# A selective-scan kernel: diagonal matrices read from spaced DRAM rows, softplus summed by accumulating DMAs, y added to DRAM by a DMA

## The chip, the core and the metric

The kernel runs on one core of one Trainium2 chip. The metric is the device time of one execution in microseconds, as the median of several. The engines named below are TensorE (PE, with its weight loads shown apart as PEld), VectorE (DVE), ScalarE (ACT), GpSimd (POOL) and SyncE (SP), which here only issues DMAs. Each engine executes its own instructions in the order in which they are written, and waits on semaphores for the others.

## The reference, cut to what matters

Two layers act on an image of 256 x 256 tokens with 128 channels: an attention over rows, then a state-space layer in the manner of VMamba. The change lies in the second layer, in its selective scan. Four scans (rows forward, columns forward, and both backward) run over the 65,536 tokens, with 256 inner channels d and 16 states n:

```python
delta = jax.nn.softplus(dts + dt_bias)
def step(h, inp):
    d_t, x_t, B_t, C_t = inp
    dA = jnp.exp(d_t[..., None] * As)
    h = dA * h + (d_t * x_t)[..., None] * B_t[:, :, None, :]
    y = jnp.einsum('bkdn,bkn->bkd', h, C_t)
    return (h, y)
...
y = out_y[:, 0] + inv_y[:, 0] + wh_y + invwh_y
```

So for each token: a step size delta for each channel, a decay exp(delta A) for each channel and state, an input delta x B, a recurrence, and a sum over the 16 states weighted with C. The four directions are added up token by token.

## The kernel before, in words

Seven stages follow one another: statistics, a norm, attention, the convolution, a transposition of one array in DRAM, the four scans, and the output. The scans take most of the time and they alone are changed. Everything is float32.

A scan is cut into 64 blocks of 1024 tokens (`TB`); four scans make 256 blocks. In each block there are 32 units, one for each state m (16) and each half h of the channels (2 x 128). A unit is written as s in the program, with s = 2m + h. The program is ordered by hand (`manual_schedule`): `body` (L908) walks over the units, and in each unit it writes for each engine the work that is due.

- `recur` (L853): DVE runs the recurrence of one unit as one scan instruction over 1024 tokens (L858), from the decay `da` and the input `mm` (a PSUM tile). After h = 1, DVE saves the last state (L863), and POOL multiplies both halves of the result `hs` with C of this state (`cc`, L865).
- `turn` (L841): PE makes the input of the unit one ahead, delta x B, as channels on partitions and tokens along the row. For four of the eight groups of 128 tokens (`DJ = NJ // 2`) it multiplies delta x (`dxt`) by a diagonal matrix `dg` that has B on its diagonal (L846). For the other four, ACT has scaled `dxt` by B into `but` and PE only transposes (L848). There are two such PSUM tiles (`mms`), so `turn` of unit u + 1 can run once the scan of unit u - 1 is over.
- `scale` (L830): ACT makes `dg` (the identity, scaled row by row, L833) and `but` (L835), six units ahead, in rings of four.
- `decay` (L837): ACT makes `da`, four units ahead, in a ring of six.
- `collect` (L869): PE transposes the products `hs` back and adds them up in PSUM tiles `y` over the 16 states, at least three states (`LAG`) behind, at most ten transposes in a unit unless `share` (L906) names another number.
- `fetch` (L825): SP loads `cc` for a state (512 KB, one row spread over 128 partitions) into a ring of four. It waits until POOL has multiplied with the buffer's former contents.
- `begin` (L737): the pieces that prepare the next block while the present one is scanned, each with the unit at which it is written. In units 6 and 8 PE forms the pre-activation of delta (`rate`, L745, into a tile of `mms`) and ACT takes its absolute value (`size`). Then ACT forms exp(-|v|), the logarithm log(1 + e), and a rounding correction (units 9 to 12). POOL adds the three parts (L780, L777, units 11 to 14). In units 18 and 20 PE forms the pre-activation again, and DVE adds max(v, 0) to give `delta` (L783). In units 22 and 24 PE transposes `delta` (`turn_rate`, L785) and DVE multiplies by x (`times_x`, L792) to give `dxt`.
- `evict` (L893): in units 6 and 8 of the next block, DVE adds the PSUM sums of a block to `yb` (L898). That buffer was loaded from `y` in DRAM at unit 16 (L948) and is stored back by SP (L902).

The order of SP's queue is the order of writing; a DMA that has to wait holds up those written after it.

Of the kernel before, what the change touches and what calls it, by code (L numbers as in the profile page):

```python
# [29 lines left out]
AF = mybir.ActivationFunctionType  # L30
ALU = mybir.AluOpType
# [588 lines left out]
def scans(tc, io, c):  # L620
# [19 lines left out]
    with tc.tile_pool(name="e_w", bufs=1) as wp, tc.tile_pool(name="e_1", bufs=1) as sb1, tc.tile_pool(  # L640
# [11 lines left out]
        def ring(name, n, shape, pool=wp):  # L652
            return [pool.tile(shape, F32, name=f"{name}{i}") for i in range(n)]

        DJ = NJ // 2
        xks = ring("xk", 1, [P, NJ, DI])

        dts = ring("dt", 1, [P, TB])
# [7 lines left out]
        bus = ring("but", 4, [P, NJ - DJ, DI])  # L666
# [18 lines left out]
        class Block:  # L685
# [40 lines left out]
            def load_tokens(self):  # L726
                nc.sync.dma_start(out=self.as_rows(self.bt), in_=self.rows(io["bk"][self.S.k]))
                nc.sync.dma_start(out=self.as_rows(self.xk), in_=self.rows(io["xk"]))

            def advance(self, now, after):  # L730
                if self.pieces is None:
                    self.pieces = begin(self)
                while self.pieces and self.pieces[0][:2] <= (now, after):
                    _, _, f, *args = self.pieces.pop(0)
                    f(*args)

        def begin(B):  # L737
# [19 lines left out]

            def size(h):
                nc.scalar.activation(B.e[:, h, :], B.pu[h], AF.Abs)  # L759

            def exp():
                nc.scalar.activation(B.e, B.e, AF.Exp, scale=-1.0)
# [10 lines left out]

                nc.scalar.activation(B.w, B.w, AF.Identity, scale=-1.0, bias=1.0)

            def less(h):
                nc.gpsimd.tensor_tensor(B.lw[:, h, :], B.lw[:, h, :], B.w[:, h, :], ALU.add)  # L777

            def log1p(h):
                nc.gpsimd.tensor_tensor(B.lw[:, h, :], B.lw[:, h, :], B.e[:, h, :], ALU.add)  # L780

            def softplus(h):
                nc.vector.scalar_tensor_tensor(B.delta[:, h, :], B.pu[h], 0.0, B.lw[:, h, :], ALU.max, ALU.add)  # L783

            def turn_rate(i):  # L785
                B.pt = mm().rearrange("p (j d) -> p j d", d=DI)
# [5 lines left out]
            def times_x(i):  # L792
# [5 lines left out]
                    ALU.mult,  # L798
                )

            return [
                (6, False, rate, 0),
                (6, True, size, 0),
                (8, False, rate, 1),
                (8, True, size, 1),
                (9, True, exp),
                (10, True, log),
                (11, True, log1p, 0),
                (11, True, one_plus),
                (12, True, log1p, 1),  # L810
                (12, True, rest),
                (13, True, less, 0),
                (14, True, less, 1),

                (18, False, rate, 0),
                (18, True, softplus, 0),
                (20, False, rate, 1),
                (20, True, softplus, 1),
                (22, False, turn_rate, 0),
                (22, True, times_x, 0),  # L820
                (24, False, turn_rate, 1),
                (24, True, times_x, 1),
            ]

        def fetch(B, m):  # L825
            nc.sync.dma_start(out=ccs[m % 4], in_=B.S.C[m : m + 1, B.where()].partition_broadcast(P))

        def scale(B, m, h):  # L830
            dg, bu = dgs[m % 4], bus[m % 4]
            for j in range(h * DJ // 2, (h + 1) * DJ // 2):
                nc.scalar.activation(dg[:, j, :], c.ident, AF.Copy, scale=B.bt[:, B.slot(j), m : m + 1])  # L833
                at = B.slot(DJ + j)
                nc.scalar.activation(bu[:, j, :], B.dxt[:, DJ + j, :], AF.Copy, scale=B.bt[:, at, m : m + 1])  # L835

        def decay(B, m, h):  # L837
            da = das[((B.n * DS + m) * NH + h) % DA]
# [2 lines left out]
        def turn(B, m, h):  # L841
            d1 = B.d1 = mm()
            dg, bu = dgs[m % 4], bus[m % 4]
            hc = slice(h * P, (h + 1) * P)
            for j in range(DJ):
                nc.tensor.matmul(d1[:, j * P : (j + 1) * P], B.dxt[:, j, hc], dg[:, j, :], start=True, stop=True)  # L846
            for j in range(DJ, NJ):
                nc.tensor.transpose(d1[:, j * P : (j + 1) * P], bu[:, j - DJ, hc], c.ident)  # L848
            d1s.append(d1)

        d1s = []
# [41 lines left out]
        def evict(B, after, part):  # L893

            n = NJ // PB // 2
            for g in range(part * n, (part + 1) * n):
                to = B.y[:, g * PB : (g + 1) * PB, :]
                nc.vector.tensor_tensor(to, to, pys[g], ALU.add)  # L898
                if after:
                    after.free.add(g)  # L900
            if part == 1:
                nc.sync.dma_start(out=B.rows(io["y"]), in_=B.as_rows(B.y))  # L902

        U = NH * DS

        share = {6: 0, 7: 8, 8: 0, 18: 3, 20: 3, 22: 5, 24: 5}  # L906

        def body(blocks, before, after):  # L908

# [11 lines left out]
            def do(f, u):  # L921
                if at(u):
                    f(*at(u))

            if before is None:
                blocks[0].load()
                blocks[0].load_tokens()
                blocks[0].advance(U, True)
                blocks[0].free = set(range(NJ // PB))
                blocks[1].load()  # L930
                for m in range(4):
                    fetch(blocks[0], m)
                for u in range(3 * NH):
                    do(scale, u)
                for u in range(4):
                    do(decay, u)
                do(turn, 0)
            for x, B in enumerate(blocks):
                nxt = at_hand.get(x + 1)
                for s in range(U):  # L940
                    u = x * U + s
                    m, h = divmod(s, NH)
                    if s == 0 and nxt:
                        nxt.load_tokens()
                    if s == 21 and x + 2 in at_hand:
# [12 lines left out]
                    if nxt:  # L958
                        nxt.advance(s, True)
                    do(decay, u + 4)  # L960
                    if u == 0:
                        nc.scalar.preload_act_table_set("natural_log_exp_and_others")
                    do(scale, u + 3 * NH)
                    if h == NH - 1 and at(u + 1 + 3 * NH):
                        fetch(*at(u + 1 + 3 * NH)[:2])
            if not after:
                waiting.extend((*at(u), j) for u in range(own * U - LAG * NH, own * U) for j in range(NJ))
                collect_some(len(waiting))
                for part in range(2):
                    evict(blocks[-1], None, part)  # L970
            assert not waiting


# [24 lines left out]
def output(tc, io, c):  # L998
# [73 lines left out]
    "dc1": (KD // 2 * RC, NT),  # L1072
    "dcT": (KD // 2 * RC, NT),
    "y": (NT, DI),
}


# [56 lines left out]
```

## Time and profile before

| what | value |
|---|---|
| median of 3 runs | 28445.06 us (28438.65 to 28445.41) |
| profiled execution, first to last instruction | 28447.5 us |
| stretch of the four scans (4744 to 27715 us) | 22971 us, that is 89.7 us for each of 256 blocks |
| busy in that stretch: PE, DVE, ACT, POOL | 21791, 21224, 22282, 21572 us |
| the same for one block | 85.1, 82.9, 87.0, 84.3 us |
| share of the 16 DMA engines, and rate, in that stretch | 0.39, 131 GB/s |
| granted TensorE clock, mean of the span | 0.965 |

The profiled execution is within 0.01% of the median of the runs, so its times can be set against the runs directly. Busy time is the time in which an instruction of an engine is under way; successive ACT instructions overlap a little, so that the distance from start to start (the pitch) is the shorter measure of what one costs.

### The profile page before, as it was taken

Reading aid. Unit: us, or ns where it says so; the run is one execution under the profiler, and the core shown is the slowest. Engines: PE = TensorE matmul, PEld = TensorE weight load, DVE = VectorE, ACT = ScalarE, POOL = GpSimd, SP = SyncE. Lnnn points to the kernel's source line nnn. Section 1 sums busy time; section 2 is a strip of 40 time slices with the busy share of each in tenths; the row PEclk is TensorE's granted clock in tenths of the full one; section 3 lists DMA queues with packets and bytes.
Section 4 is the critical chain, followed back from the end, with each engine's and each line's share of the span. In section 5 each row is a group of like instructions: output and inputs, shape, how many; then the busy total and the mean of one; then the engine's idle time right before and its main releaser. Section 6 shows DMA issues by size and latency. Waiting matters only on the chain. (4 is left out here: it accounts for less than half of the span.)

```text
span 28447.5 us, 528099 instructions
## 1 busy us (share of the span) xinstructions
PE 26610.1 (94%) x196490; PEld 22529.2 (79%) x196490; DVE 24922.2 (88%) x24253; ACT 25332.4 (89%) x49673; POOL 22944.4 (81%) x10118
## 2 busy tenths in 40 slices
PE   8999996999999999999999999999999999999998
PEld 3555444888888888888888888888888888888884
DVE  4777665999999999999999999999999999999987
ACT  6875224999999999999999999999999999999987
POOL 2443002999999999999999999999999999999983
PEclk9999998999999999999999999999999999999999
DMA  5112345433433333333334333333333333333335
GB/s 206 55 50 71 111 116 115 132 132 129 133 130 133 132 131 132 132 131 132 128 132 133 131 133 132 131 132 129 132 132 130 133 132 129 132 130 132 133 132 172
DMA packets 1923996, 3630.07 MB, mean 128 GB/s; under 512 B 532297, under 2 KB 1240009, under 8 KB 1889490
## 3 DMA queue, kind: packets, MB, share of 16 engines
q1 hardware_dynamic: 1424722, 3339.77, 34.6%
q10 hardware_dynamic: 496640, 255.88, 3.2%
q8 instruction: 1568, 25.69, 0.4%
q14 instruction: 1066, 8.73, 0.1%
HBM read 3002.42 MB, written 592.84 MB: 126 GB/s over the span
## 5 line engine op out<-in xcount | busy, mean ns | idle before, releaser
L865 POOL TENSOR_TENSOR hs<-hs,cc 128x1024 f32<-128x1024 f32 x8192 | 19202.5, 2380 | 1346.1 <-DVE state L863 679.9
L858 DVE TENSOR_TENSOR_SCAN hs<-da,state,mm 128x1024 f32<-128x1024 f32 x8192 | 18976.6, 2340 | 1465.4 <-PE mm L848 1074.7
L846 PE MATMUL mm<-dg,dxt 128*128 128x128 f32 x65536 | 9305.0, 287 | 1065.1 <-DVE hs L858 886.1
L846 PEld LDWEIGHTS mm<-dg,dxt 128*128 128x128 f32 x65536 | 8328.4, 199 | 2257.9 <-DVE hs L858 1897.8
L839 ACT ACTIVATE da<-delta,A 128x1024 f32<-128x1024 f32 x8192 | 9328.4, 1139 | 112.2 <-PEq L984 76.0
L617 PE MATMUL y<-ident,hs 128*128 128x128 f32 x65536 | 8511.4, 275 | 1.4 <-POOL hs L865 1.4
L835 ACT ACTIVATE but<-dxt,bt 128x256 f32<-128x256 f32 x16384 | 8150.2, 497 | 11.4 <-DVE dxt L794 11.4
L617 PEld LDWEIGHTS y<-ident,hs 128*128 128x128 f32 x65536 | 7494.1, 143 | 1.9 <-POOL hs L865 1.9
L833 ACT ACTIVATE dg<-ident,bt 128x128 f32<-128x128 f32 x16384 | 6393.1, 390 | 0.2
L848 PE MATMUL mm<-ident,but 128*128 128x128 f32 x32768 | 5092.5, 280 | 0.0
L848 PEld LDWEIGHTS mm<-ident,but 128*128 128x128 f32 x32768 | 4011.4, 146 | 0.0
L750 PE MATMUL mm<-dt,dtw 9*128 9x512 f32 x4096 | 2033.0, 615 | 265.9 <-DMA bt<-mid_bk 184.5
L385 POOL TENSOR_TENSOR an<-ex,rs 128x1024 f32<-128x1024 f32 x512 | 970.2, 1895 | 1024.5 <-PE tp L394 566.3
L780 POOL TENSOR_TENSOR lw<-lw,e 128x1024 f32<-128x1024 f32 x512 | 1207.7, 2384 | 336.3 <-ACT lw L766 336.3
L750 PEld LDWEIGHTS mm<-dt,dtw 9*128 9x128 f32 x4096 | 680.7, 184 | 959.5 <-issue 733.3
L500 POOL MEMSET pad<- 128x10 f32 x32 | 3.7, 117 | 1650.0 <-PE ps L537 1639.9
L777 POOL TENSOR_TENSOR lw<-lw,w 128x1024 f32<-128x1024 f32 x512 | 1202.9, 2375 | 0.0
L537 PE MATMUL ps<-pad,w 128*128 128x512 f32 x2048 | 954.8, 610 | 161.0 <-ACT xi L525 161.0
L372 ACT ACTIVATE ex<-sc,nm 128x256 f32<-128x256 f32 x2048 | 1013.7, 499 | 0.4
L759 ACT ACTIVATE e<-mm 128x1024 f32<-128x1024 f32 x512 | 524.7, 1025 | 522.1 <-PE mm L750 521.9
L355 DVE CUSTOM_DVE_ANT_0 sc<-ps,bias 128x256 f32<-128x256 f32 x2048 | 746.2, 421 | 117.3 <-PE ps L340 117.3
L394 PEld LDWEIGHTS tp<-ident,an 128*128 128x128 f32 x4096 | 467.5, 141 | 470.7 <-POOL an L385 235.1
(137 smaller groups left out, 18522.4 us busy)
## 6 DMA issues: line engine op xcount, KB each, us to landing
cc<-mid_dc SPq DMA_DIRECT2D x2048, 512.0 KB
cc<-mid_dcT SPq DMA_DIRECT2D x2048, 512.0 KB
xk<-mid_xk SPq DMA_DIRECT2D x256, 1024.0 KB
yb<-mid_y SPq DMA_DIRECT2D x256, 1024.0 KB
mid_y<-yb SPq DMA_DIRECT2D x256, 1024.0 KB
xt<-mid_xT SPq DMA_DIRECT2D x64, 1024.0 KB
mid_xk<-xk ACTq DMA_DIRECT2D x32, 2048.0 KB
mid_y<-y ACTq DMA_DIRECT2D x32, 2048.0 KB
```

Source lines behind the costliest of these rows:

```text
L372: nc.scalar.activation(exs[u][:, x, :], scs[u][:, e, jt, :], AF.Exp, scale=-1.0, bias=nms[u][:, e, jt : jt + 1], accum_out=sms[u][:, x : x ...
L617: nc.tensor.matmul(out, in_, c.ident, is_transpose=True, start=start, stop=stop, skip_group_check=True)
L750: nc.tensor.matmul(pu[:, q : q + T], dtw[0 : DR + 1, k, h * P : (h + 1) * P], B.dt[0 : DR + 1, q : q + T], start=True, stop=True,)
L777: nc.gpsimd.tensor_tensor(B.lw[:, h, :], B.lw[:, h, :], B.w[:, h, :], ALU.add)
L780: nc.gpsimd.tensor_tensor(B.lw[:, h, :], B.lw[:, h, :], B.e[:, h, :], ALU.add)
L833: nc.scalar.activation(dg[:, j, :], c.ident, AF.Copy, scale=B.bt[:, B.slot(j), m : m + 1])
L835: nc.scalar.activation(bu[:, j, :], B.dxt[:, DJ + j, :], AF.Copy, scale=B.bt[:, at, m : m + 1])
L839: nc.scalar.activation(da, B.delta[:, h, :], AF.Exp, scale=A[:, B.S.k * NH + h, m : m + 1])
L846: nc.tensor.matmul(d1[:, j * P : (j + 1) * P], B.dxt[:, j, hc], dg[:, j, :], start=True, stop=True)
L848: nc.tensor.transpose(d1[:, j * P : (j + 1) * P], bu[:, j - DJ, hc], c.ident)
L858: nc.vector.tensor_tensor_scan(o, d0, d1, state[:, m, h : h + 1], ALU.mult, ALU.add)
L865: nc.gpsimd.tensor_tensor(hs[:, x, :], hs[:, x, :], ccs[m % 4], ALU.mult)
```

## The change

1. **Diagonals.** `DJ` becomes 3: the groups 0, 2 and 4 go by a diagonal, the other five by scaling and a transposition. ACT no longer makes `dg`. Instead a new piece `spread` is written in units 10, 13, 16 and 19 for four states each: ACT copies 12 columns of B into a zeroed tile `z` at a spacing of 128 elements, and SP writes the whole tile (128 rows of 1664 elements, 0.85 MB) to DRAM (`apart`, two copies by the parity of the block). Reading that with a row step one element shorter than the row shifts each row by one element, which yields the three diagonal matrices of a state: `diagonal`, one SP load of 0.2 MB for each state, into the same ring `dg`.
2. **Softplus.** ACT writes max(v, 0) into `delta` by Relu right after the Abs, and the three further parts are added onto `delta` by three DMAs that accumulate, issued from POOL in units 12, 15 and 18, 1 MB each from SBUF to SBUF. The second `rate`, POOL's four additions and DVE's `softplus` are gone.
3. **y.** The sums are copied out of PSUM by ACT instead of being added by DVE, and a DMA from POOL in unit 10 (`add_y`) accumulates them onto `y` in DRAM. The load of `yb` at unit 16 and SP's store are gone.

```diff
-        DJ = NJ // 2
+        DJ = 3
+        BJ = NJ - DJ
+        by_diagonal, by_scale = (0, 2, 4), (1, 3, 5, 6, 7)
+        GS = 4
+        ZL = P * (GS * DJ + 1)
...
+        zs = ring("z", 1, [P, ZL])
+        for z in zs:
+            nc.vector.memset(z, 0.0)
...
             def size(h):
                 nc.scalar.activation(B.e[:, h, :], B.pu[h], AF.Abs)
+                nc.scalar.activation(B.delta[:, h, :], B.pu[h], AF.Relu)
...
-            def less(h):
-                nc.gpsimd.tensor_tensor(B.lw[:, h, :], B.lw[:, h, :], B.w[:, h, :], ALU.add)
-
-            def log1p(h):
-                nc.gpsimd.tensor_tensor(B.lw[:, h, :], B.lw[:, h, :], B.e[:, h, :], ALU.add)
-
-            def softplus(h):
-                nc.vector.scalar_tensor_tensor(B.delta[:, h, :], B.pu[h], 0.0, B.lw[:, h, :], ALU.max, ALU.add)
+            def add(name):
+                nc.gpsimd.dma_start(out=B.delta, in_=getattr(B, name), accum_op=ALU.add)
...
+            def spread(g):
+                z = zs[0]
+                first, step = B.slot(by_diagonal[0]), B.slot(by_diagonal[1]) - B.slot(by_diagonal[0])
+                nc.scalar.copy(
+                    z[:, P - 1 : P - 1 + GS * DJ * P].rearrange("p (m j q) -> p j m q", j=DJ, q=P)[:, :, :, 0],
+                    B.bt[:, first : first + step * (DJ - 1) + 1 : step, g * GS : (g + 1) * GS],
+                )
+                nc.sync.dma_start(out=B.apart(g), in_=z)
+
+            pieces = [(10 + 3 * g, True, spread, g) for g in range(DS // GS)]
+            return sorted(pieces + [
                 (6, False, rate, 0),
                 (6, True, size, 0),
                 (8, False, rate, 1),
                 (8, True, size, 1),
                 (9, True, exp),
                 (10, True, log),
-                (11, True, log1p, 0),
                 (11, True, one_plus),
-                (12, True, log1p, 1),
                 (12, True, rest),
-                (13, True, less, 0),
-                (14, True, less, 1),
-
-                (18, False, rate, 0),
-                (18, True, softplus, 0),
-                (20, False, rate, 1),
-                (20, True, softplus, 1),
+                (12, True, add, "lw"),
+                (15, True, add, "e"),
+                (18, True, add, "w"),
                 (22, False, turn_rate, 0),
...
+        def diagonal(B, m):
+            of = B.apart(m // GS)
+            of = bass.AP(of.tensor, of.offset + P - 1 + m % GS * DJ * P, ((ZL - 1, P), (1, DJ * P)))
+            nc.sync.dma_start(out=dgs[m % 4].rearrange("p j q -> p (j q)"), in_=of)
...
-            for j in range(h * DJ // 2, (h + 1) * DJ // 2):
-                nc.scalar.activation(dg[:, j, :], c.ident, AF.Copy, scale=B.bt[:, B.slot(j), m : m + 1])
-                at = B.slot(DJ + j)
-                nc.scalar.activation(bu[:, j, :], B.dxt[:, DJ + j, :], AF.Copy, scale=B.bt[:, at, m : m + 1])
+            for x in range(h * BJ // 2, (h + 1) * BJ // 2):
+                j = by_scale[x]
+                nc.scalar.activation(bu[:, x, :], B.dxt[:, j, :], AF.Copy, scale=B.bt[:, B.slot(j), m : m + 1])
...
-                nc.vector.tensor_tensor(to, to, pys[g], ALU.add)
+                nc.scalar.copy(to, pys[g])
...
+        def add_y(B):
+            nc.gpsimd.dma_start(out=B.rows(io["y"]), in_=B.as_rows(B.y), accum_op=ALU.add)
...
-        share = {6: 0, 7: 8, 8: 0, 18: 3, 20: 3, 22: 5, 24: 5}
+        share = {6: 0, 7: 8, 8: 0, 22: 5, 24: 5}
...
-                    if s == 16:
-                        nc.sync.dma_start(out=B.as_rows(B.y), in_=B.rows(io["y"]))
...
+                    if x - 1 in at_hand and s == 10:
+                        add_y(at_hand[x - 1])
...
                     do(scale, u + 3 * NH)
+                    if h == 0 and at(u + 3 * NH):
+                        diagonal(*at(u + 3 * NH)[:2])
                     if h == NH - 1 and at(u + 1 + 3 * NH):
                         fetch(*at(u + 1 + 3 * NH)[:2])
```

More of the change, by code (lines that the diff above doesn't have):

```diff
@@ L665, in scans @@
         dgs = ring("dg", 4, [P, DJ, P])
-        bus = ring("but", 4, [P, NJ - DJ, DI])
+        bus = ring("but", 4, [P, BJ, DI])
+        zs = ring("z", 1, [P, ZL])
+        for z in zs:
+            nc.vector.memset(z, 0.0)
         das = ring("da", DA, [P, TB])
@@ L728, in load_tokens, with apart @@
                 nc.sync.dma_start(out=self.as_rows(self.xk), in_=self.rows(io["xk"]))
+            def apart(self, g):
+                return io["apart"][self.b % 2, g]
             def advance(self, now, after):
@@ L799, in times_x @@
                 )
-            return [
+            def spread(g):
[8 more added lines that the diff above has]
+            return sorted(pieces + [
                 (6, False, rate, 0),
@@ L822, in begin @@
                 (24, True, times_x, 1),
-            ]
+            ], key=lambda x: x[:2])
         def fetch(B, m):
             nc.sync.dma_start(out=ccs[m % 4], in_=B.S.C[m : m + 1, B.where()].partition_broadcast(P))
+        def diagonal(B, m):
+            of = B.apart(m // GS)
+            of = bass.AP(of.tensor, of.offset + P - 1 + m % GS * DJ * P, ((ZL - 1, P), (1, DJ * P)))
+            nc.sync.dma_start(out=dgs[m % 4].rearrange("p j q -> p (j q)"), in_=of)
         def scale(B, m, h):
-            dg, bu = dgs[m % 4], bus[m % 4]
-            for j in range(h * DJ // 2, (h + 1) * DJ // 2):
-                nc.scalar.activation(dg[:, j, :], c.ident, AF.Copy, scale=B.bt[:, B.slot(j), m : m + 1])
-                at = B.slot(DJ + j)
-                nc.scalar.activation(bu[:, j, :], B.dxt[:, DJ + j, :], AF.Copy, scale=B.bt[:, at, m : m + 1])
+            bu = bus[m % 4]
+            for x in range(h * BJ // 2, (h + 1) * BJ // 2):
+                j = by_scale[x]
+                nc.scalar.activation(bu[:, x, :], B.dxt[:, j, :], AF.Copy, scale=B.bt[:, B.slot(j), m : m + 1])
         def decay(B, m, h):
@@ L844, in turn @@
             hc = slice(h * P, (h + 1) * P)
[L845 to L848, printed above, removed]
+            for x, j in enumerate(by_diagonal):
+                nc.tensor.matmul(d1[:, j * P : (j + 1) * P], B.dxt[:, j, hc], dg[:, x, :], start=True, stop=True)
+            for x, j in enumerate(by_scale):
+                nc.tensor.transpose(d1[:, j * P : (j + 1) * P], bu[:, x, hc], c.ident)
             d1s.append(d1)
@@ L897, in evict @@
                 to = B.y[:, g * PB : (g + 1) * PB, :]
-                nc.vector.tensor_tensor(to, to, pys[g], ALU.add)
+                nc.scalar.copy(to, pys[g])
                 if after:
                     after.free.add(g)
-            if part == 1:
-                nc.sync.dma_start(out=B.rows(io["y"]), in_=B.as_rows(B.y))
+        def add_y(B):
+            nc.gpsimd.dma_start(out=B.rows(io["y"]), in_=B.as_rows(B.y), accum_op=ALU.add)
         U = NH * DS
-        share = {6: 0, 7: 8, 8: 0, 18: 3, 20: 3, 22: 5, 24: 5}
+        share = {6: 0, 7: 8, 8: 0, 22: 5, 24: 5}
         def body(blocks, before, after):
@@ L932, in body @@
                     fetch(blocks[0], m)
+                for m in range(3):
+                    diagonal(blocks[0], m)
                 for u in range(3 * NH):
@@ L970, in body @@
                     evict(blocks[-1], None, part)
+                add_y(blocks[-1])
             assert not waiting
@@ L1074 @@
     "y": (NT, DI),
+    "apart": (2, 4, P, P * 13),
 }
```

## The prediction

> **What bounds the kernel now.** I read the page's busy shares and costliest groups first, then the timeline of one block engine by engine, then the waits of SP's queue.
>
> ```profile
> PE 26610.1 (94%) x196490; PEld 22529.2 (79%) x196490; DVE 24922.2 (88%) x24253; ACT 25332.4 (89%) x49673; POOL 22944.4 (81%) x10118
> L865 POOL TENSOR_TENSOR hs<-hs,cc 128x1024 f32<-128x1024 f32 x8192 | 19202.5, 2380 | 1346.1 <-DVE state L863 679.9
> L858 DVE TENSOR_TENSOR_SCAN hs<-da,state,mm 128x1024 f32<-128x1024 f32 x8192 | 18976.6, 2340 | 1465.4 <-PE mm L848 1074.7
> L780 POOL TENSOR_TENSOR lw<-lw,e 128x1024 f32<-128x1024 f32 x512 | 1207.7, 2384 | 336.3 <-ACT lw L766 336.3
> ```
>
> Nothing has slack to speak of: in the scans all four engines are busy for 83 to 87 of 89.7 us a block. DVE sets the pace, because it has the chain that can't be reordered: a pair of scans with the state saved has a pitch of 4.73 us, so 2.365 a unit and 75.7 us for 32. The rest of a block must be gaps between scans. Its timeline on DVE shows them (start, length, engine, line):
>
> ```profile
> 12055.84 2.35 DVE L858 TENSOR_TENSOR_SCAN hs<-da,state,mm 128x1024 f32<-128x1024 f32 x1
> 12058.34 1.22 DVE L783 SCALAR_TENSOR_TENSOR delta<-mm,lw 128x1024 f32<-128x1024 f32 x1
> 12059.95 2.35 DVE L858 TENSOR_TENSOR_SCAN hs<-da,state,mm 128x1024 f32<-128x1024 f32 x1 [0.39 <-PE mm L848]
> ...
> 12062.41 2.35 DVE L858 TENSOR_TENSOR_SCAN hs<-da,state,mm 128x1024 f32<-128x1024 f32 x1
> 12064.67 1.20 DVE L783 SCALAR_TENSOR_TENSOR delta<-mm,lw 128x1024 f32<-128x1024 f32 x1
> 12067.16 2.35 DVE L858 TENSOR_TENSOR_SCAN hs<-da,state,mm 128x1024 f32<-128x1024 f32 x1 [1.29 <-PE mm L848]
> ...
> 12069.82 2.35 DVE L858 TENSOR_TENSOR_SCAN hs<-da,state,mm 128x1024 f32<-128x1024 f32 x1
> 12072.08 1.20 DVE L794 TENSOR_TENSOR dxt<-mm,xk 128x1024 f32<-128x1024 f32 x1
> 12073.92 2.35 DVE L858 TENSOR_TENSOR_SCAN hs<-da,state,mm 128x1024 f32<-128x1024 f32 x1 [0.64 <-PE mm L848]
> ```
>
> Six times a block (units 6, 8, 18, 20, 22, 24) a rate or a transposed delta takes one of the two PSUM tiles `mm`. PE can then turn the next unit only when the present scan has ended, and DVE waits for one turn: the scans stand 4.1 us apart instead of 2.3. The 1.2 us instruction in the gap is mostly inside that wait. 75.7 plus six gaps of 1.75 to 2.4 is the 88 to 89 us of a block away from the loop's ends (`mid_y` is stored at 19 points within 1610.7 us, 89.5 apart, loop ends included).
>
> **The change, part by part, for one block.**
>
> *Second rate and softplus gone (units 18, 20).* Both gaps vanish. Start to start they exceed 2.365 by 1.75 and 2.39 us above; in the next block (12144.79 to 12148.89, 12151.35 to 12156.28) by 1.74 and 2.57. Mean of the pairs: 4.2 us off DVE's path.
>
> *Evict off DVE (units 6, 8).* Two adds of 0.67 lie in each gap that a rate makes anyway: 12023.34 to 12027.47 is 4.13, as wide as the gaps with one instruction in them. I gain nothing there. The gap is the cover; without the rate the adds would be 2.6 us.
>
> *One diagonal fewer.* Four products load weights for 0.97 us a turn, four transposes for 0.47, so one swap saves 0.125 in each of the four gaps left: 0.5 us. PE also sheds 32 x 0.125 and two rates of 1.98, all beside DVE.
>
> *ACT.* From the timeline's pitches:
>
> ```profile
> 12058.02 0.39 ACT L833 ACTIVATE dg<-ident,bt 128x128 f32<-128x128 f32 x1
> 12058.31 0.49 ACT L835 ACTIVATE but<-dxt,bt 128x256 f32<-128x256 f32 x1
> 12058.71 0.39 ACT L833 ACTIVATE dg<-ident,bt 128x128 f32<-128x128 f32 x1
> ```
>
> A dg costs 0.29, a but 0.40. Off: 64 x 0.29 = 18.6. On: 16 but x 0.40 = 6.4; two Relu as the Abs, 0.92 each; four evictions as the output's 128x512 copy, 0.585; four spreads as the output's 128x8 Sqrt, 0.30. Net -6.9, from 87.0 to 80.1: cover for ACT's new waits on `z`, and no gain while DVE needs 84. Relu holds its `mm` 0.92 longer; PE needs that tile only for the turn after next, which the trace has 1.4 us later than the first, so nothing, or up to 0.9 twice were it tight.
>
> *POOL and the accumulating DMAs.* Off: four additions, 9.4 us. On: four issues of a length c that the trace of before never shows, since POOL issues no DMA there. Below: SP's issue of 1 MB took 0.38 (L728). Above: a whole POOL instruction, 2.38. I take 1.0, nearer the issue. The landing time D of 1 MB added SBUF to SBUF isn't shown either. The nearest row is a cc load of 512 KB, issued at 12041.58, by stretches of half a microsecond (busy share of DMA, GB/s last):
>
> ```profile
> 12042.50:12043.00 0.50, 1.00 0.69 188
> 12043.00:12043.50 0.50, 1.00 0.98 369
> ```
>
> It starts 0.9 after its issue and moves at 369 GB/s, ending about 2.9 after issue. One MB at that rate moves in 2.8. An addition reads two operands and writes one: one pass gives D = 0.9 + 2.8 + 0.5 for its end, say 4.4; two passes 7.0; three passes 9.9. I take 7.0, two reads on one path.
>
> Now the chain, which is where I choose. Each add must wait on the one before, since they write the same delta, and the wait sits in POOL's queue ahead of the products `hs` of later units; behind those wait PE's collects, SP's `fetch` and, behind it, `diagonal`. The trace's POOL times of this block:
>
> ```profile
> 12041.92 4.73 POOL L865 TENSOR_TENSOR hs<-hs,cc 128x1024 f32<-128x1024 f32 x2 [0.36 <-DVE state L863]
> 12046.60 4.73 POOL L780 TENSOR_TENSOR lw<-lw,e 128x1024 f32<-128x1024 f32 x2
> 12051.27 4.72 POOL L865 TENSOR_TENSOR hs<-hs,cc 128x1024 f32<-128x1024 f32 x2
> ```
>
> POOL works 4.7 us per state, as long as DVE's 4.73, so it can't catch up. It ends state 4 at 12041.5. Then by program order: y's issue (c), state 5, lw's issue (c), states 6 and 7, e's issue (c). 41.5 + 3 x 4.7 + 3c = 55.6 + 3c. w may start when state 8 is done (4.7) and e has landed (D), and lands c + D later: 55.6 + 4c + 2D for D above 4.7; with c = 1, D = 7 that is 12073.6. PE wants delta in unit 22, 0.82 us after that scan starts (12069.82, first transposes at 12070.64). With the two gaps gone unit 22 starts at 12036.91 + 12 x 2.365 = 12065.3, so PE asks at 12066.1. Stall: 4c + 2D - 10.5 = 7.5 us. PE then holds the turn of unit 23 behind it, and DVE stands.
>
> By the Trainium skill, "DMA: Bandwidth & Descriptors", Rules for kernel authors, an accumulate must be issued from GpSimd and nothing guards its bytes until its semaphore is in, which is the rule against this change: three adds on one tile can only go one after another. Its section Bandwidth has 6.15 us of movement for 1 MB from HBM, slower than this trace's 369 GB/s row; with about 1 us to the first byte, as its specifications give, D would be some 7.2 (an estimate from that page) and the stall 7.9 instead of 7.5.
>
> *Diagonals' DMAs.* Each waits on SP behind a fetch, and fetches already follow POOL:
>
> ```profile
> SPq L826 <- POOL hs L865: 5050.9, 1074, 8.9
> ```
>
> This is what was in the waits of 6000 us of scans. The diagonal of state m + 4 is issued after POOL ends state m, at least 4.8 after its scan; PE needs it some 12.4 after that scan (5 units and the 0.6 that a turn can start late). Landing takes 0.9 + 1.4 (cc ahead of it) + 0.6 + 0.5 plus its own issue, some 3.8, and 2.3 more behind a 0.85 MB `z`. That leaves 1.5 to 3.8 us for POOL's lag, which my chain puts at 3 before unit 18. Tight, but its lateness falls into the same stall, so I add nothing; alone it could cost what rival two prices. Bytes: 11.6 MB a block now (131 GB/s x 88.7); + 3.4 z + 3.1 diagonals + 4.2 adds - 2.1 y = 20.2, or 28.6 with additions three-fold, 77 us at 369 GB/s: it fits, not by much.
>
> *Sum.* -4.2 - 0.5 + 7.5 = +2.8 us a block, x 256 = +717, on a profiled 28447.5 (the median is 2.4 lower): 29165 us. In general 256 x (4c + 2D - 15.2).
>
> **Rivals.**
>
> *One: the adds land in time, and it is faster.* The same formula changes sign at D = 5.6 with c = 1. With the lower bounds, c = 0.4 and D = 4.4, the last add lands at 12066.3, the stall is 0.2 and 256 x -4.5 gives 27300; with c = 0.7, D = 5, 27830. For it: 369 GB/s, DMA idle for 61% of the stretch, 9.4 us of POOL's work gone. Against: it needs an addition that costs hardly more than a copy, in the busiest stretch of the DMA queues.
>
> *Two: SP's queue.* If POOL lags over 3 us, the diagonals behind the four `z` come some 2 us late each, at L846 of units 18 to 24, apart from delta's wait: 8 - 4.7 = +3.3 a block, 29290. For it: the fetch's wait above. Against: four buffers, and a lag of at most 9.6 us harmed nothing before (but nothing on PE's path hung on it then).
>
> *Three: POOL's issue is long.* For y in the row scans the rows are of 1 KB, 1024 of them. With c = 2.4 throughout and D = 7 the sum is +8.4 a block, 30600; with both upper bounds 32080.
>
> **How the numbers follow.** Forecast (delta late at unit 22) 0.44; rival one 0.39; rivals two and three together 0.12; 0.05 that gain and stall cancel within 0.2%, which is about what a measurement of this kernel can tell from no change. Faster 0.39, same 0.05, slower 0.56. The point is the forecast's, 29165. Its own range, D from 5.8 to 9 and c from 1 to 1.5, is 28550 to 30700. The range takes in rival one down to its lower bounds and the other two to c = 2.4: 27350 to 30800.
>
> **What would show it.** Right: DVE or PE idle at `turn_rate` (L790 before) by 5 to 10 us a block, released by a DMA into delta; POOL waiting on the first and second adds; softplus gaps gone; DVE's scans unchanged at 2.34. Wrong: that idle under 4 us, a block of 84 to 86 us, or idle at the diagonal product instead. ACT should drop to some 80 us a block, POOL to 79, DMA share rise to 0.6 or more. If POOL's issues show below 0.5 us and the adds land within 5, rival one holds.

## The result, and the profile after

| | before | after |
|---|---|---|
| median | 28445.24 us of 4 runs (28438.65 to 28445.60) | 32552.83 us of 4 runs (32546.85 to 32591.05) |
| profiled execution | 28447.5 us | 32556.0 us |
| granted TensorE clock, mean | 0.965 | 0.901 |
| DMA share and rate, 6000 us of scans from 12000 us | 0.39, 131 GB/s | 0.65, 190 GB/s |

The ratio is 1.1447, 95% interval 1.1431 to 1.1463: slower by 4108 us, 16.0 us for each of the 256 blocks, where 2.8 were forecast. The sign was right, the size was not, and the time lies outside the range.

The first lines of the page of after, with busy time, share of the span and instructions, and then its groups at issue (busy us, mean ns of one, idle time before them and what ended most of it):

```profile
PE 26482.5 (81%) x186250; PEld 22604.4 (69%) x186250; DVE 23770.1 (73%) x22718; ACT 23698.1 (73%) x39945; POOL 21604.1 (66%) x10118
...
L871 DVE TENSOR_TENSOR_SCAN hs<-da,state,mm 128x1024 f32<-128x1024 f32 x8192 | 18938.6, 2339 | 4926.2 <-PE mm L861 3819.5
...
L859 PE MATMUL mm<-dg,dxt 128*128 128x128 f32 x49152 | 8021.0, 304 | 3651.7 <-DMA dg<-mid_apart 2629.9
...
L795 PE MATMUL mm<-ident,delta 128*128 128x128 f32 x4096 | 762.8, 348 | 1729.3 <-DMA delta<-w 1729.1
L799 DVE TENSOR_TENSOR dxt<-mm,xk 128x1024 f32<-128x1024 f32 x512 | 620.4, 1212 | 1915.4 <-PE mm L795 1870.0
...
L809 ACT COPY z<-bt 128x12 f32<-128x12 f32 x1024 | 215.1, 210 | 1994.3 <-DMA mid_apart<-z 1993.5
```

No engine is near full any more. DVE's own account closes: its busy time fell by 1152 us (24922.2 to 23770.1), its idle time rose by 5261 (3525.3 to 8785.9), and the difference is the loss. The scans are as long as ever (2339 ns), but the idle before them grew from 1465.4 to 4926.2 us, and there are 1915.4 more before `times_x` (L799). Behind both stands PE, and PE waits for two DMAs: the last add, `delta<-w` (1729 us, 6.8 a block, the wait that was forecast), and the diagonals (2630 us, 10.3 a block, the wait that was put at nothing).

The issues of the page's last part (count, KB, median us to landing, which the profile counts from the start of the issue to the semaphore that tells of the landing):

```profile
delta<-lw POOLq DMA_DIRECT2D x256, 1024.0 KB, 14.3
delta<-e POOLq DMA_DIRECT2D x256, 1024.0 KB, 11.6
delta<-w POOLq DMA_DIRECT2D x256, 1024.0 KB, 9.6
```

The forecast had 7.0 for each. That was the right figure for a quiet machine. Ahead of the first block of the scans, from 4759 us on, there is no y and no diagonal under way; three writes of `z` run beside the adds, and `cc` loads from 4777 us on, beside the last. The same view of that stretch has

```profile
delta<-lw POOLq DMA_DIRECT2D x1, 1024.0 KB, 7.1
delta<-e POOLq DMA_DIRECT2D x1, 1024.0 KB, 7.3
delta<-w POOLq DMA_DIRECT2D x1, 1024.0 KB, 7.5
```

In e7, a run below without diagonals and `z`, the adds of `e` and `w` at this place have no other transfer beside them, and land in

```profile
delta<-e POOLq DMA_DIRECT2D x1, 1024.0 KB, 7.0
delta<-w POOLq DMA_DIRECT2D x1, 1024.0 KB, 6.9
```

The prediction's estimate of some 7.2 from the Trainium skill, "DMA: Bandwidth & Descriptors", Bandwidth, agrees with these five in number, and not with the three of the running scans. But that page's 6.15 us are for a plain load from HBM, and plain copies at this place, beside writes of `z`, landed in 5.8 and 4.9 us (the first two of e3 below); so the agreement says little about adds.

One block in the timeline of after, POOL first (start, length, engine, line; in brackets the idle time before it):

```profile
14053.42 1.57 POOL L916 DMA_DIRECT2D mid_y<-yb  x1
14059.07 1.54 POOL L788 DMA_DIRECT2D delta<-lw  x1
...
14075.74 0.87 POOL L788 DMA_DIRECT2D delta<-e  x1 [5.79 <-DMA delta<-lw]
...
14087.62 0.87 POOL L788 DMA_DIRECT2D delta<-w  x1 [6.27 <-ACT but L848]
```

and PE:

```profile
14072.99 1.62 PE L859 MATMUL mm<-dg,dxt 128*128 128x128 f32 x6 [7.50 <-DMA dg<-mid_apart]
...
14096.19 1.94 PE L795 MATMUL mm<-ident,delta 128*128 128x128 f32 x8 [10.73 <-DMA delta<-w]
```

POOL stands still twice, as each add waits for the one ahead: y's add is issued at 14053, 5.7 us ahead of `lw`; `lw` then takes 16.7 us until `e` may go, `e` 11.9 until `w` may go (the bracket there names ACT's `but`, which does not write delta; by the program the issue waits for `e`), and `w` some 8.6 until PE starts. PE loses 10.73 us for it at 14096, but it had lost 7.50 in the same block already, at 14073, to a diagonal.

### The profile page after: what moved, and what is told of

Read it like the earlier page. It is cut to its first block, busy times and chain, and to the rows that moved or that the text cites. A ratio compares the mean times of both kernels' runs of the same rounds, so it can differ in the third digit from the quotient of the medians.

```text
span 32556.0 us, 508089 instructions
## 1 busy us (share of the span) xinstructions
PE 26482.5 (81%) x186250; PEld 22604.4 (69%) x186250; DVE 23770.1 (73%) x22718; ACT 23698.1 (73%) x39945; POOL 21604.1 (66%) x10118
## 5 line engine op out<-in xcount | busy, mean ns | idle before, releaser
L871 DVE TENSOR_TENSOR_SCAN hs<-da,state,mm 128x1024 f32<-128x1024 f32 x8192 | 18938.6, 2339 | 4926.2 <-PE mm L861 3819.5
L878 POOL TENSOR_TENSOR hs<-hs,cc 128x1024 f32<-128x1024 f32 x8192 | 19589.7, 2524 | 4076.4 <-DVE state L876 1737.5
L859 PE MATMUL mm<-dg,dxt 128*128 128x128 f32 x49152 | 8021.0, 304 | 3651.7 <-DMA dg<-mid_apart 2629.9
L859 PEld LDWEIGHTS mm<-dg,dxt 128*128 128x128 f32 x49152 | 6802.0, 209 | 4891.4 <-issue 2332.5
L848 ACT ACTIVATE but<-dxt,bt 128x256 f32<-128x256 f32 x20480 | 8992.7, 499 | 956.2 <-PE mm L861 945.7
L861 PE MATMUL mm<-ident,but 128*128 128x128 f32 x40960 | 6354.3, 290 | 0.0
L861 PEld LDWEIGHTS mm<-ident,but 128*128 128x128 f32 x40960 | 5248.5, 152 | 0.0
L795 PE MATMUL mm<-ident,delta 128*128 128x128 f32 x4096 | 762.8, 348 | 1729.3 <-DMA delta<-w 1729.1
L799 DVE TENSOR_TENSOR dxt<-mm,xk 128x1024 f32<-128x1024 f32 x512 | 620.4, 1212 | 1915.4 <-PE mm L795 1870.0
L795 PEld LDWEIGHTS mm<-ident,delta 128*128 128x128 f32 x4096 | 633.6, 182 | 1803.4 <-issue 1801.9
L911 ACT COPY yb<-y 128x512 f32<-128x512 f32 x1024 | 547.2, 583 | 1083.6 <-PE y L617 1083.1
L760 PE MATMUL mm<-dt,dtw 9*128 9x512 f32 x2048 | 1086.6, 652 | 185.4 <-DMA bt<-mid_bk 184.2
## 6 DMA issues: line engine op xcount, KB each, us to landing
delta<-lw POOLq DMA_DIRECT2D x256, 1024.0 KB, 14.3
delta<-e POOLq DMA_DIRECT2D x256, 1024.0 KB, 11.6
```

The lines of the kernel that those rows point to most:

```text
L760: nc.tensor.matmul(pu[:, q : q + T], dtw[0 : DR + 1, k, h * P : (h + 1) * P], B.dt[0 : DR + 1, q : q + T], start=True, stop=True,)
L795: nc.tensor.transpose(B.pt[:, j, h * P : (h + 1) * P], B.delta[:, h, at : at + P], c.ident)
L848: nc.scalar.activation(bu[:, x, :], B.dxt[:, j, :], AF.Copy, scale=B.bt[:, B.slot(j), m : m + 1])
L861: nc.tensor.transpose(d1[:, j * P : (j + 1) * P], bu[:, x, hc], c.ident)
L871: nc.vector.tensor_tensor_scan(o, d0, d1, state[:, m, h : h + 1], ALU.mult, ALU.add)
L878: nc.gpsimd.tensor_tensor(hs[:, x, :], hs[:, x, :], ccs[m % 4], ALU.mult)
```

## The experiments

Theory A stands for the prediction's mechanism (adds one after another, the last one late), theory B for the diagonals' transfers as a cause of their own. "Before" on the same chip was 28440.4 to 28447.1 us throughout. Runs with one time are taken as known to about 0.2%, since the five times of e12 lie within 0.16%. The cuts of the diffs are shortened; `...` marks what is left out.

**The whole change with one part undone.** In e1 the softplus, in e2 the diagonals are as before:

```diff
 e1:
-                (12, True, add, "lw"), (15, True, add, "e"), (18, True, add, "w"),
+                (11, True, log1p, 0), (12, True, log1p, 1), (13, True, less, 0), (14, True, less, 1),
+                (18, False, rate, 0), (18, True, softplus, 0), (20, False, rate, 1), (20, True, softplus, 1),
 ...
 e2:
-        DJ = 3
+        DJ = 4
 ...
-            pieces = [(10 + 3 * g, True, spread, g) for g in range(DS // GS)]
+            pieces = []
 ...
+                nc.scalar.activation(dg[:, x, :], c.ident, AF.Copy, scale=B.bt[:, B.slot(by_diagonal[x]), m : m + 1])
-                        diagonal(*at(u + 3 * NH)[:2])
 ...
```

> The changed kernel (32553 us) with the softplus of before: POOL's additions, the second rate, DVE's softplus; no DMA adds onto delta. Diagonals from DRAM and y by DMA stay. Theory A (the serial adds are the root: delta is late at unit 22, and POOL, held by them, makes the fetches and so the diagonals late): the wait of the delta transposes (1729 us) goes and most of the diagonals' wait (2630 us) with it; the two gaps come back (+4.2 us a block, 1075 us). About 28600 us, between 28200 and 29300. Theory B (the diagonals are late by themselves, behind cc and z on SP's queue): their wait stays near 2600 us and the time is 30500 or more.

> The changed kernel with four diagonals made by ACT as before; no z tile, no DRAM copy of it, no diagonal loads (6.5 MB a block less traffic). The DMA adds onto delta and y by DMA stay. Theory A: the last add still lands late, though faster on emptier queues (8 us instead of 10 to 14); with landing 8 us for each and 0.9 us per issue the forecast's formula gives 256 x (3.6 + 16 - 15.2) = +1130, so 29600 us, between 29000 and 30800. Theory B: nearly all of the loss was the diagonals, so 27700 to 28600 us.

Without the adds (e1) 30330.16 us: 1884 above before, with PE's wait for diagonals still at 1722.7 us. That lies between the two theories' expectations: it is not the adds alone. Without the diagonals (e2) 29910.94 us: 1465 above before. Of its groups, the transposes of delta:

```profile
L792 PE MATMUL mm<-ident,delta 128*128 128x128 f32 x4096 | 762.7, 348 | 2038.4 <-DMA delta<-w 2038.4
```

Here the forecast's stall stands by itself: 2038.4 / 256 = 8.0 us a block, 7.5 in the forecast. That the two figures lie so close is in part luck. The forecast's landings D of 7.0 were already times from the issue, and it added the issue c once more for `e` and for `w`, 2 us too much; on the other side the landings here are 12.1, 7.9 and 7.0. With these, and no second c, its chain has `lw` issued at 47.2 on its clock, `e` at 59.3, `w` at 67.2, landed at 74.2, against 66.1 when PE asks: a stall of 8.1. The stall less the two gaps gained (4.2) is 3.8 a block, and the run lost 5.7; the 1.9 between are in no term of the forecast.

The diagonals make the difference from e2 to after, 2642 us, and it is most of the 3388 that the forecast lacked.

**Each part alone, on the kernel before.** e5 has the y part only, e6 the diagonals, e7 the softplus; each is before with that item of the change's diff and nothing else.

> Before, with the y part of the change alone: sums copied out by ACT, added to DRAM by a DMA from POOL. If DVE's adds lay inside the gaps of the rates, as the forecast said, nothing is gained on DVE; ACT gets four copies of 0.585 us a block on top of 87.0 of 89.7 busy, and POOL one issue of 1.4. Expected 28445 to 28950, most likely +1.4 us a block, 28800. If the evictions did lie on DVE's path: 27800 or less.

> Before, with the diagonals part alone. Theory B (diagonals late by themselves): about the 30330 us of the run with the softplus undone, less what y's DMA put on the queues, 29900 to 30300. If they are only late because of the adding DMAs: 28100 to 28700, ACT being relieved by some 12 us a block.

> Before, with the softplus part alone. The first add no longer queues behind y's add on POOL's ring: its landing falls from 12.1 us (in the run with the diagonals undone) to some 7 to 8, the others stay at 7 to 8. With c = 0.9 (three issues, not four) and D = 7.5 the formula's stall is 2.7 + 15 - 10.5 = 7.2 us a block; less 4.2 that is +3.0 a block: 29200 us, between 28900 and 29700. If the chain of three adds doesn't matter without the other two parts: 27400 to 28400.

- e5, y alone: 28465.95, 23 us above before, within the expectation. Taking DVE's evictions out of the gap gained nothing.
- e7, softplus alone: 30135.16, +1692, 6.6 a block, above the 28900 to 29700 expected.
- e6, diagonals alone: 31213.28, +2771, 10.8 a block, above both expectations. e1, which differs from it by y's part, is 883 us faster: there SP's queue has neither the load of `yb` nor the store of y.

The three sum to 17.5 a block; the whole change has 16.0, so they overlap by little in the sum. e7's chain in its timeline, POOL and then PE:

```profile
12120.11 0.85 POOL L785 DMA_DIRECT2D delta<-lw  x1
...
12130.04 1.16 POOL L785 DMA_DIRECT2D delta<-e  x1
...
12140.73 0.88 POOL L785 DMA_DIRECT2D delta<-w  x1 [4.81 <-ACT dg L844]
```

```profile
12149.03 1.94 PE L792 MATMUL mm<-ident,delta 128*128 128x128 f32 x8 [8.18 <-DMA delta<-w]
```

`lw` is hidden behind two states, as the forecast assumed; `e` and `w` are not. With this run's landings (`e` 11.2, beside the 1 MB load of `yb` that SP issues 1 us behind it, and `w` 7.3) and no issue of y, the forecast's chain has `lw` issued at 46.2, `e` at 56.6, `w` at 67.8, landed at 75.1: a stall of 9.0. Measured: 9.1 us of PE's wait a block (2335.4 us in all). Less the two gaps that makes +4.9; measured are 6.6, so here too 1.8 are in no term. What they are was not separated; DVE's scans in e7 wait 330 us, 1.3 a block, for ACT's `da`.

e6 has no add at all and loses more. Its groups and then the longest of the waits of SP's queue in 6000 us of scans (total, times, longest):

```profile
L869 PE MATMUL mm<-dg,dxt 128*128 128x128 f32 x49152 | 7774.5, 297 | 3750.2 <-DMA dg<-mid_apart 2841.4
...
L814 ACT COPY z<-bt 128x12 f32<-128x12 f32 x1024 | 206.8, 202 | 3353.9 <-DMA mid_apart<-z 3353.8
```

```profile
SPq L845 <- POOL hs L888: 3885.4, 853, 13.8
```

The timeline of e6 shows how they hang together, SP's queue, then ACT, then PE:

```profile
14069.81 0.34 SPq L845 DMA_DIRECT2D cc<-mid_dc  x1
...
14071.30 0.34 SPq L818 DMA_DIRECT2D mid_apart<-z  x1
...
14074.87 0.54 SPq L850 DMA_DIRECT2D dg<-mid_apart  x1
14080.04 0.32 SPq L818 DMA_DIRECT2D mid_apart<-z  x1
```

```profile
14079.80 0.21 ACT L814 COPY z<-bt 128x12 f32<-128x12 f32 x1 [13.25 <-DMA mid_apart<-z]
```

```profile
14080.36 1.62 PE L869 MATMUL mm<-dg,dxt 128*128 128x128 f32 x6 [8.22 <-DMA dg<-mid_apart]
```

SP issues nothing from 14060.97 to 14069.81 (the `cc` load waits for POOL), then within 5.1 us two `cc` loads, the load of `yb`, a write of `z` and two diagonals: 3.2 MB in one queue, a diagonal last. From 14074.87 it stands again until 14080.04: the next write of `z` waits for ACT's copy, and ACT has stood for 13.25 us, with its `da` and `but` behind that copy, until the former write of `z` landed. Read together, PE, late for a diagonal, makes DVE late, DVE POOL, and POOL the next `cc` load, behind which the next diagonal is queued: a loop. The next two runs break it.

**Is it the order on the queues or the bytes?** e9 is e6 with each diagonal written one unit earlier, ahead of the `cc` load; e10 is e9 with `z` issued from ACT's queue:

```diff
 e9 (and e4):
-                    if h == 0 and at(u + 3 * NH):
-                        diagonal(*at(u + 3 * NH)[:2])
                     if h == NH - 1 and at(u + 1 + 3 * NH):
+                        diagonal(*at(u + 1 + 3 * NH)[:2])
                         fetch(*at(u + 1 + 3 * NH)[:2])
 ...
 e10, besides:
-                nc.sync.dma_start(out=B.apart(g), in_=z)
+                nc.scalar.dma_start(out=B.apart(g), in_=z)
```

> The diagonals part alone (31213 us), each diagonal load written one unit earlier and ahead of the fetch of its state. Theory: what makes diagonals late is SP's order, behind a fetch that waits for POOL; moved ahead it is released by POOL one state (4.7 us) earlier. Then PE's wait for diagonals falls from 2841 us to below 900 and the time to 28300 to 29300. Rival: z, which SP also issues in order, holds the loads up as well (SP waits for ACT's copy, ACT's copy for the z before it): the wait stays above 1500 us, the time above 29700.

> As the run before it, and z issued from ACT's queue, right behind the copy that fills it, so nothing on SP waits for ACT and z's 0.85 MB lie on another ring. If z on SP was the rest of the lateness: the diagonals' wait below 400 us, ACT's wait for z below 300 us, and the time 28100 to 28600 (the six gaps of the rates are still there, each shorter by 0.12 us). If traffic alone makes the loads late, no change against the run before it.

e9: 29219.05; PE's wait for diagonals fell from 2841 to 693 us. ACT still waited 3415 us for `z`, and DVE now waited for ACT's `da` (1133). e10: 28457.09 against 28447.11 before, and its groups are

```profile
L881 DVE TENSOR_TENSOR_SCAN hs<-da,state,mm 128x1024 f32<-128x1024 f32 x8192 | 18957.5, 2340 | 1451.0 <-PE mm L871 961.8
...
L869 PE MATMUL mm<-dg,dxt 128*128 128x128 f32 x49152 | 7712.3, 296 | 1399.5 <-DVE hs L881 1107.3
```

The 2771 us are gone, with the same bytes and more of them in a second: from 12000 to 18000 us the rate is 204 GB/s at a DMA share of 0.61, where e6 had 181 at 0.55. So the loss of the diagonals alone came from the order on SP's queue (the diagonals behind `cc`, and `z` among them), not from the bytes. Nor is there a gain: PE waits for DVE again, DVE's idle before the scans is what it was before (1465.4), and the time that ACT saves, 5836 us busy in those 6000 before and 5049 now, is not on the path.

**The same cures in the whole change.** e4 moves the diagonal only, e11 moves the diagonal and `z` both:

> The changed kernel with each diagonal load written one unit earlier, ahead of the fetch of the same state instead of behind it, so it no longer waits for POOL's product or for 512 KB of cc. Theory B, or A with the wait on SP as the link: the wait of PE on the diagonals (2630 us) falls below 600 us and the time to 30000 to 31000 us. If what makes them late is the traffic itself (z, adds, cc on the same engines), the wait stays above 1500 us and the time above 31700.

> The whole change with both reorderings. The diagonals' wait should go as in the run before it, while the three adds stay in series: with their landing at 10 us (emptier SP ring, same traffic) the stall is 4 + 20 - 10.5 = 13.5 us, less 4.7, +8.8 a block: 30700 us, between 30000 and 31300, nearly all of its loss in the wait for delta (2500 to 3500 us). If diagonals and adds were one stall, the time would stay at 31900.

e4: 31896.75, e11: 31917.01; both save some 650 us and no more. e11 was expected at 30000 to 31300; its time is what the rival there had, 31900 if diagonals and adds were one stall. Of its groups, the transposes of delta:

```profile
L795 PE MATMUL mm<-ident,delta 128*128 128x128 f32 x4096 | 763.0, 349 | 3279.3 <-DMA delta<-w 3279.2
```

PE's wait for the diagonals fell to 817.8 us in e11 (1446 in e4), and its wait for `delta` rose from 1729 to 3279 (2887 in e4). The adds take as long as before (15.3, 11.2 and 9.1 us in e11): whatever arrives sooner at unit 22 waits there longer. So in the whole change the two waits stand one behind the other, and the later sets the end. The forecast's chain with each run's landings gives +12.0 a block for e11 and +11.7 for e4; measured are 13.6 and 13.5.

**Whose traffic makes the adds land late?** e3 turns the three adds into plain copies in the order w, e, lw, and so leaves out the sum; e8 copies `z` to DRAM in the first four blocks of each scan only, and so leaves out the diagonals of the later ones; e15 has y as before.

```diff
 e3:
-                nc.gpsimd.dma_start(out=B.delta, in_=getattr(B, name), accum_op=ALU.add)
+                nc.gpsimd.dma_start(out=B.delta, in_=getattr(B, name))
 ...
 e8:
-                nc.sync.dma_start(out=B.apart(g), in_=z)
+                if B.b < 4:
+                    nc.sync.dma_start(out=B.apart(g), in_=z)
 e15:
-                nc.scalar.copy(to, pys[g])
+                nc.vector.tensor_tensor(to, to, pys[g], ALU.add)
-            nc.gpsimd.dma_start(out=B.rows(io["y"]), in_=B.as_rows(B.y), accum_op=ALU.add)
+            nc.sync.dma_start(out=B.rows(io["y"]), in_=B.as_rows(B.y))
 ...
```

> The changed kernel, the three DMAs onto delta as plain copies of the same size from the same queue (w, then e, then lw), so the three parts are left out of the sum and delta ends as the last copy. If an addition costs about two passes of a copy, landing falls from 14, 12 and 10 us to some 7 and the time to 30500 or less. If queues shared with the other transfers set the landing, it stays within 2 us of the adds and the time within 700 us of 32553.

> The changed kernel, with the tile z copied to DRAM in the first four blocks of a scan alone, so B's diagonals of later blocks are left out (old ones are read); 3.4 MB a block less traffic, all else as it was, the diagonal loads too. If z's traffic ahead of cc and the diagonals on SP's ring is what makes these late, the diagonals' wait falls from 2630 to under 1000 us, and ACT's wait for z is gone: 30500 to 31300 us, the adds still late. If the order on SP behind POOL is the cause: wait above 2000 and time above 31800.

> The whole change with y as before (DVE adds, SP loads and stores it). The first add has nothing ahead of it on POOL's ring: its landing falls from 14.3 us to 10 or 11; the next add is issued that much earlier, so the time falls by 256 x 3 = 800 us or so, to 31300 to 32100, although y's two transfers are back on SP's ring. If y's add had no part in it: 32400 to 32900.

| run | time, us | landings of the three, in order of issue, us | PE waits for delta, for diagonals, us |
|---|---|---|---|
| after | 32552.83 | 14.3, 11.6, 9.6 | 1729, 2630 |
| e3, copies | 30645.63 | 10.3, 8.4, 7.1 | 898, 1840 |
| e8, `z` rarely | 30668.67 | 12.1, 8.7, 7.0 | 1131, 1809 |
| e15, y as before | 31834.71 | 11.3, 12.9, 10.5 | 922, 2866 |
| e2, no diagonals | 29910.94 | 12.1, 7.9, 7.0 | 2038, none |

e3 came between its two expectations: an add lands 2.5 to 4 us later than a copy in the same place of the chain, and the copies still take 7.1 to 10.3 us. Without the writes of `z` each add lands 2 to 3 us sooner (PE's wait for diagonals falls less than was expected, to 1809 us); without y's add ahead of it in POOL's queue the first lands 3 us sooner, while `e` then runs beside the load of `yb` and lands 1.3 later. So a good part of the lateness of the adds is that of their company, and part is that they add.

**Versions meant to be faster.** e12 drops the second rate with no DMA at all: DVE takes max(v, 0) from the first rate's PSUM and adds the rest from SBUF. e13 is e10 with the second rate gone, Relu on ACT, POOL's additions kept, and one DMA that adds `lw` in unit 14. e14 has POOL's last additions and the add in unit 12.

```diff
 e12, against before:
+                nc.vector.tensor_scalar(B.delta[:, h, :], B.pu[h], 0.0, None, ALU.max)
 ...
-                nc.vector.scalar_tensor_tensor(B.delta[:, h, :], B.pu[h], 0.0, B.lw[:, h, :], ALU.max, ALU.add)
+                nc.vector.tensor_tensor(B.delta[:, h, :], B.delta[:, h, :], B.lw[:, h, :], ALU.add)
-                (18, False, rate, 0), (20, False, rate, 1),
 e13, against e10:
+                nc.scalar.activation(B.delta[:, h, :], B.pu[h], AF.Relu)
 ...
-                (18, False, rate, 0), (18, True, softplus, 0), (20, False, rate, 1), (20, True, softplus, 1),
+                (14, True, add, "lw"),
 ...
 e14, against e13:
-                (13, True, less, 0), (14, True, less, 1), (14, True, add, "lw"),
+                (12, True, less, 0), (12, True, less, 1), (12, True, add, "lw"),
```

> Before, keeping only the idea of one rate: DVE takes max(v, 0) out of the first rate's PSUM tile in units 6 and 8 (into delta), and adds lw in units 18 and 20; no second rate, no DMA. The two gaps of units 18 and 20 (4.2 us a block) become two adds of some 1.1 to 1.2; in units 6 and 8 the gap of 1.77 now holds 1.26 + 1.1, so 0.6 more each. Net -0.6 us a block at least (28300), -1.9 at best (27950), ACT at 87.0 busy being the next limit. If DVE's add, with both inputs in SBUF, is slowed beside POOL, 28445 or slower.

> The diagonals from DRAM with both reorderings (28457 us) and of the softplus part only: Relu on ACT, no second rate, and one DMA add of the finished lw after POOL's four additions (written in unit 14). If the chain of three is the cause: POOL ends its additions where unit 20 starts, one add lands some 8.5 us later, 3.9 us after PE asks for delta; less 4.2 for the two gaps, so -0.3 a block: 28100 to 28700 us. If the adding DMA itself is the cost, 29000 or more.

> As the run before it, POOL's last two additions and the add written in unit 12, ahead of the product of state 6, so the add is issued one state (4.7 us) earlier. If the chain is the cause the add now lands before PE asks: the stall goes, the two gaps are gained, 27300 to 27800 us. Against it: POOL's lag for state 6 grows to over 10 us, and the collects and diagonals that follow POOL may stall PE; then 28200 or more, with the wait at the collects or the diagonal products, not at delta.

All three are slower than before, e13 and e14 by little: e12 29681.74 us, ratio 1.0433 (1.0418 to 1.0447); e13 28789.78, 1.0124 (1.0107 to 1.0141); e14 28818.51, 1.0137 (1.0120 to 1.0154). e12 fails on DVE itself:

```profile
L784 DVE TENSOR_TENSOR delta<-delta,lw 128x1024 f32<-128x1024 f32 x512 | 2071.3, 4046 | 14.8 <-POOL lw L778 13.0
```

A TENSOR_TENSOR of this size with one input in PSUM took 1.2 us (L799 of after, a product); this add with both in SBUF, while POOL works on `lw` and `hs`, took 4.05 on average. Two a block, 8.1 us, are more than the two gaps of 4.2 were worth. The Trainium skill, "SBUF — State Buffer", Who interferes with whom, says that a DVE instruction with two SBUF inputs contends with GpSimd's reads; this row agrees with it, though no run here took POOL's work away.

In e13 PE's wait for delta was 376.6 us, in e14 26.1: one add can be in time, which is the gain that both were expected to bring. But PE's wait for diagonals came back (706.7 and 1075.3), and ACT stood:

```profile
L860 ACT ACTIVATE da<-delta,A 128x1024 f32<-128x1024 f32 x8192 | 9337.5, 1140 | 2626.6 <-DMA yb<-mid_y 2290.3
```

This group of e13 says that ACT's idle before `da` ends with the load of `yb`, though `da` doesn't read `yb`. In the timeline of ACT such a pause of 10.1 us lies between its copy into `z` and the issue of the write of `z` in its own queue:

```profile
12003.42 0.19 ACT L815 COPY z<-bt 128x12 f32<-128x12 f32 x1
12013.33 0.33 ACTq L819 DMA_DIRECT2D mid_apart<-z  x1
12013.70 1.15 ACT L860 ACTIVATE da<-delta,A 128x1024 f32<-128x1024 f32 x1 [10.09 <-DMA yb<-mid_y]
```

So ACT stands ahead of that issue, and `da` only comes behind it. What the issue waits for was not tried and is open. No version found beats the kernel before; e5 and e10 equal it.

## Why the prediction was right and wrong

- *The adds' chain: right in its mechanism, and its term D the larger of the two steps that failed.* PE idles at `turn_rate` for a DMA into delta, POOL waits on the adds, both softplus gaps are gone, the scans are unchanged. With no diagonals about (e2) the stall was 8.0 us where 7.5 were forecast, in part by luck (see there). In the whole change the term D = 7.0 failed: it was sized from a `cc` load in a row with nothing beside it, and measured 14.3, 11.6 and 9.6. At 14.3 the first add outlasts the two states (9.4) that were to hide it and delays the second. On the forecast's clock, with c = 1 for y's issue and landings counted from the issue: `lw` issued at 47.2, `e` at 61.5, `w` at 73.1, landed at 82.7 against 66.1, a stall of 16.6 and a net of 16.6 - 4.7 = +11.9 a block, some 31490 us in all. That is 9.1 of the 13.2 a block by which the forecast was short. The timeline's c (0.6 to 1.0 from the start of POOL's issue to its next start, up to 1.2 in e7) was near enough.
- *The diagonals: the other step that failed, a term put at nothing.* "Tight, but its lateness falls into the same stall, so I add nothing." The forecast's own sign of being wrong, idle at the diagonal product, is there: 10.3 us a block. Alone the diagonals cost 10.8 us a block (e6), and with the rest 2642 us (after against e2). Rival two had the mechanism, SP's queue behind POOL, but at +3.3 a block and with POOL's lag as its condition; e6 shows that it needs no help from the adds. What the rival did not see is the loop: PE's wait for a diagonal delays POOL, POOL the `cc` load, and that the next diagonal; and a single `z` ties SP and ACT to the landing of 0.85 MB. Nor is nothing what the diagonals do to the adds: with them the three land 2.2, 3.7 and 2.6 us later (after against e2). By the chain with the landings of each (+11.9 against +3.9) this is 8.0 of the 10.3 a block that the diagonals cost in the whole change.
- *Same stall?* In part. Curing the diagonals alone returns 650 us of the whole change (e4, e11), because unit 22 waits for delta anyway. So far the forecast's sentence holds. The 16.0 us a block are then: 11.9 by the chain with measured landings, 2.6 by the order on SP's queue, and 1.5 not assigned to anything, as 1.6 to 1.9 are not in e2, e4, e7 and e11; the lower clock (0.88 against 0.97 from 12000 to 18000 us) and ACT's waits for `z` are candidates, not separated.
- *Evictions off DVE gain nothing: right* (e5, +23 us). *One diagonal fewer gains 0.5: not seen* (e10 is 10 us above before, where 128 below was forecast).
- *ACT as cover:* its busy time fell by 6.4 us a block (6.9 in the forecast, whose terms add to 6.8), but "cover for ACT's new waits on z" was too easily said: the waits reach 13 us at a time (e6; 7 in after) and hold `da`.
- *Rival one* (adds in time) fell because each landing was longer than its 5 us or less; it was 6.9 even with nothing beside it. Hiding an add is possible: e13 and e14 show one add landing in 7.6 and 7.0 us and nearly or wholly hidden. *Rival three* (long issues) fell: the issues took 0.9 to 1.6 us where it had 2.4. The DMA share (0.65) was as forecast.

## What to carry to other kernels

A load queued behind a load that waits for another engine inherits that engine's lag, and where the lag feeds back into the wait the loss grows far past the first estimate: order the queue by when things are needed, and give a staging tile that a DMA reads another queue (e10; a second buffer for it was not tried). Size a transfer's landing from the busiest stretch and from what stands ahead of it in its own queue, not from bytes over the best rate. When one of two late things is cured, look first at where the wait goes (e11), and before calling a lateness "hidden in the same stall", price it with the stall gone.

## What the runs showed of the hardware, unexpected

- An accumulating 1 MB DMA from SBUF to SBUF landed in 6.9 to 7.0 us with nothing beside it (e7, ahead of the first block) and in 7.1 to 7.5 beside writes of `z` and `cc` loads (after, at the same place); in the running scans it took 2.5 to 4 us more than a copy (after against e3).
- Issuing from POOL is not free: 0.87 us for an add, 0.58 to 0.60 for a copy (e3), and 1.26 on average for `lw`'s in after, a few us behind y's (0.87 in e7, without y's). The mean of POOL's products went from 2380 to 2524 ns; in e6, with no DMA from POOL, it is 2370.
- The granted clock goes down with the waits: 0.965 before, 0.961 in e10, 0.935 in e1, 0.901 after; and matmuls right after a stall are long, a mean of 348 ns for the transposes of delta where they wait for the add, 273 ns before.
